# A decoder layer in one core: the quarter of the down projection with eight products goes first, and half of its tokens ahead of the other quarters

## The chip, the cores and the metric

The kernel runs on one core of one Trainium2 chip. The metric is the device time of one execution in microseconds (us), lower is better. Before the change it is 2516.35 us, the median of three runs (2516.21 to 2521.84).

The core has five engines, each with its own queue of instructions in a fixed order: PE (TensorE, matrix products; PEld in a profile is its loading of weights), DVE (VectorE), ACT (ScalarE), POOL (GpSimd) and SP (SyncE, which here issues nearly all transfers between HBM and the on-chip memory). An engine that meets an instruction whose input is not there waits, and all that stands behind it waits too.

## What is computed

A decoder layer with three sublayers, each followed by a layer norm: a retention-like self attention, a cross attention, and a gated feed-forward network. The change touches the last of these:

```python
gate = jnp.einsum('bsd,hd->bsh', x, w_gate)
up = jnp.einsum('bsd,hd->bsh', x, w_up)
gated = jax.nn.silu(gate) * up
return jnp.einsum('bsh,dh->bsd', gated, w_down)
...
x = _layernorm(x + _L0_ffn_ref(x, L0_ffn_w_gate, L0_ffn_w_up, L0_ffn_w_down), axis=-1)
```

There are 800 tokens (8 x 100), the model dimension is 1024, the hidden dimension 4096, all in fp32.

## The kernel before

**Layout.** Tokens stand along the free dimension, in two halves of N = 400. The dimension of the model is 8 blocks of 128 partitions (KT = 8), the hidden dimension 32 blocks (NHID). An fp32 product is made of three matmuls on parts: each operand is split into a high part (rounded, on ACT, line 67) and a low part (the rest, on DVE, line 68), and `mm3` (lines 85 to 88) adds high x high, high x low and low x high. Hence lines 86, 87 and 88 in every view.

**Seven products for eight.** `seven` (lines 337 to 401) multiplies a 2 x 2 block of weights with a 2 x 2 block of activations (two halves of the inner dimension, two halves of the tokens) with seven block products in place of eight, in the manner of Strassen and Winograd. It needs sums of weight blocks (DVE, lines 370 to 373) and sums of activation blocks, the tiles t1 to t4 beside b11, b21 and b22. One such unit is 7 x 4 x 3 = 84 matmuls. With `into` it adds its results into the rows y (lines 355 and 364). `proj` (lines 100 to 105) is the direct way: 8 x 3 = 24 matmuls for one block of 128 outputs and one half of the tokens, so 48 for both.

**The feed-forward part.** The up projection runs over 16 units u of two hidden blocks each: gate by `seven`, silu, up by `seven`, then the gating product (line 847) and `combine` (lines 854 to 874). `combine` stores the hidden activations to HBM, split in high and low: in the long form (t1 to t4 are computed, two kinds of splits, four stores into `hd`: 1400, 200, 400 and 800 KB), or in the short form for the direct products (one split, two stores of 800 KB into `h3d`, lines 858 to 861).

The down projection takes the hidden dimension in four quarters q of eight blocks (QT = 4 units each). Three quarters (q = 0, 1, 2) go by seven products: `down_unit(q, m)` for m = 0, 2, 4, 6, with seven chunks of 1600 KB each (lines 912 to 915), loaded from `hd`. The last quarter, q = 3, goes by the direct way, in the loop at lines 971 to 979: for each half of the tokens, for each m, 24 matmuls, an addition into y (line 976), a sum over rows (`add_up`, line 253), and then the layer norm of that half (`norm_root`, lines 275 to 287, `scaled`, lines 268 to 273). The norm of half 0 lies beside the direct products of half 1; that of half 1 is the tail of the kernel.

**What sets the order.** `in_turn` (lines 403 to 414) interleaves the steps of following units, up and down units in one list, so that the products of the next unit fill the waits of the one before. The program is then ordered by a scheduler that runs a time model of its own. Within one engine the order that results is fixed.

**Where chunks lie.** `slots` (line 903) is a ring of places: one of pool fp (tag f), z, z, four big, z. In `after_up`, behind the last up unit, pools ff (the tiles r, h, t of `combine`) and sp (temporaries) are closed, the second half of y is loaded (line 897), pool hk with two more places (tag h) is opened in the memory that became free, and these two are put at the head of the ring (lines 895 to 900). The first chunk of q = 0 is loaded into f already after unit 4 (line 891), the others when the first down unit is made (line 944), the seven of the next quarter behind unit m = 2 (lines 952 and 953). The four tiles for the direct products are taken after m = 2 of q = 2 (lines 955 to 958).

Buffers that matter: raw weights `wst` 3, split weights `w` 4, accumulator banks a 3, s 4, v 1.

Of the kernel before, what the change touches and what calls it, by code (L numbers as in the profile page):

```python
# [11 lines left out]
ALU = mybir.AluOpType  # L12
# [8 lines left out]
KT = D // P  # L21
QT = KT // 2
# [11 lines left out]
UNITS = NHID // 2  # L34
# [5 lines left out]
def decoder_layer(ctx, tc, xT, cT, w1, wo1, w2, wo2, wc, w3, wd, gw, qw, kw, trig, dec, mask, out):  # L40
    nc = tc.nc

    def sbuf(name, bufs, side=None):
        return tc.tile_pool(name=name, bufs=bufs, side=side, reuse_waits="tile")
# [8 lines left out]
    def bank(tag):  # L53
        return ps.tile([P, 512], F32, tag=tag, name=tag, bufs=banks[tag])

    def f32(ap):
        return ap.bitcast(F32)
# [4 lines left out]
    def split(dst, src):  # L62

        split2(dst[:, 0], dst[:, 1], src)

    def split2(hi, lo, src):
        nc.scalar.copy(hi, src)  # L67
        nc.vector.tensor_tensor(lo, src, f32(hi), ALU.subtract)  # L68
# [21 lines left out]
    def mmw(acc, w, k, rh, rl, start, stop):  # L90
        c = slice(k * P, (k + 1) * P)
        mm3(acc, w[:, 0, c], w[:, 1, c], rh, rl, start, stop)
# [3 lines left out]
    def acc_tag():  # L96
        turn[0] += 1
        return "as"[turn[0] % 2]

    def proj(w, z, n=N, tag="a"):  # L100
        acc = bank(tag)[:, :n]
        for k in range(KT):
            t = z[k // QT]
            mmw(acc, w, k, t[:, 0, k % QT, :n], t[:, 1, k % QT, :n], k == 0, k == KT - 1)
        return acc
# [54 lines left out]
    hd = dr.tile([QT - 1, 7, P, 2, QT, N], FR, name="hd")  # L160
    h3d = dr.tile([4, P, 2, QT, N], FR, name="h3d")
# [89 lines left out]
    def add_up(s1, y, m):  # L251
        if m > 0:
            nc.vector.tensor_tensor(s1, y[:, 0] if m == 1 else s1, y[:, m], ALU.add)
# [69 lines left out]
    def load_raw(src):  # L323
        st = wp.tile([P, KT * P], F32, tag="wst", name="wst", bufs=3)
        if isinstance(src, list):
            for i, s in enumerate(src):
                nc.sync.dma_start(out=st[:, i * H:(i + 1) * H].rearrange("p (u c) -> p u c", u=QT), in_=s)
        else:
            nc.sync.dma_start(out=st, in_=src)
        return st  # L330

    def w_split(src):
        w = wp.tile([P, 2, KT * P], FR, tag="w", name="w", bufs=4)
        split(w, src)
        return w
# [67 lines left out]
    def in_turn(units):  # L403

        at = sorted((7 * i + 2 * j, i) for i in range(len(units)) for j in range(-1, 7))
        started = {}
        for _, i in at:
            make, then = units[i]
            if i not in started:
                started[i] = make()  # L410
            try:
                next(started[i])
            except StopIteration:
                then()


    with sbuf("l1", 2) as p:
# [120 lines left out]
        def unit(h, i, then):  # L538
            c = {}
            return (lambda: seven(p, w1[h, i], w1[h, i + 1], zb, "ass", temp, c.__setitem__),  # L540
                    lambda: then(h, [(hb, c[name]) for hb, name in zip(HB, C)]))
# [76 lines left out]
    with sbuf("l2", 2) as p:  # L618
        for kv in range(NKV):
            for i0, i1 in ((0, 4), (4, 6)) if kv == 0 else ((0, 2), (2, 4), (4, 6)):  # L620
# [8 lines left out]
                for half in range(2):  # L629
                    bs = slice(half * NB, (half + 1) * NB)  # L630
                    for i in range(i0, i1):
                        acc = proj(ws[i - i0], z1[half], tag=acc_tag())
# [22 lines left out]
    with sbuf("cx", 2) as p, sbuf("c1", 1) as p1:  # L655
# [6 lines left out]
        for b in range(B):  # L662
            if b > 0:
                load_context(b)
            for kv in range(NKV):
                if early:
                    kall, row = early.pop(0)
                else:
# [7 lines left out]
                q = p.tile([P, 4, 2, T], FR, tag="q", name="q")  # L676
                nc.sync.dma_start(out=f32(q).rearrange("p h l t -> p h (l t)"),
                                  in_=f32(qd[kv, :, :, b]).rearrange("h p l t -> p h (l t)"))
# [27 lines left out]
                for j, c in enumerate(ORDER):  # L706
                    rows, n, t0 = (R6, N6, T6) if c == 6 else (P, N, 0)
# [35 lines left out]
                for j in (1, 0, 2, 3, 4, 5, 6):  # L743
                    c = ORDER[j]
                    n = N6 if c == 6 else N
# [26 lines left out]

    fp = ctx.enter_context(sbuf("fp", 1, "right"))
    z2p = ctx.enter_context(sbuf("z2", 1, "right"))
    zb = {}
# [57 lines left out]
    ORDER7 = ("b11", "b21", "b22", "t1", "t3", "t2", "t4")  # L835
# [18 lines left out]
    def combine(u, r):  # L854
        h = ff.tile([P, 7, N], FR, tag="h", name="h")
        q, j = u // QT, u % QT
        if q == QT - 1:
            split2(h[:, 0:4], r, r)
            nc.sync.dma_start(out=f32(h3d[:, :, 0, j]).rearrange("c p n -> p c n"), in_=f32(h[:, 0:4]))
            nc.sync.dma_start(out=f32(h3d[:, :, 1, j]).rearrange("c p n -> p c n"), in_=r)  # L860
            return
        t = ff.tile([P, 4, N], F32, tag="t", name="t")
        pairs = r.rearrange("p (i x) n -> p i x n", x=2)
        nc.vector.tensor_tensor(t[:, 0:2], pairs[:, :, 1], r[:, 0:2], ALU.subtract)
        nc.vector.tensor_tensor(t[:, 2], r[:, 3], t[:, 0], ALU.subtract)
        nc.vector.tensor_tensor(t[:, 3], r[:, 2], t[:, 2], ALU.subtract)
        split2(h[:, 3:7], t, t)
        split2(h[:, 1:3], r[:, 2:4], r[:, 2:4])
        split2(h[:, 0], r[:, 0], r[:, 0])
        to = lambda a, b, l: f32(hd[q, a:b, :, l, j]).rearrange("c p n -> p c n")  # L870
        nc.sync.dma_start(out=to(0, 7, 0), in_=f32(h))
        nc.sync.dma_start(out=to(0, 1, 1), in_=r[:, 0:1])
        nc.sync.dma_start(out=to(1, 3, 1), in_=r[:, 2:4])
        nc.sync.dma_start(out=to(3, 7, 1), in_=t)
# [13 lines left out]

    def after_up(u):
        if u == QT:  # L890
            load_chunk(0, down_order[:1])
        elif u == UNITS - 2:
            load_y(fp)
        elif u == UNITS - 1:
            ffpool.__exit__(None, None, None)
            sppool.__exit__(None, None, None)
            load_y(ctx.enter_context(sbuf("yy", 1)))
            pools.append(sbuf("hk", 1))
            hk = pools[0].__enter__()
            slots[0:0] = [lambda: hk.tile([P, 2, QT, N], FR, tag="h", name="h", bufs=2)] * 2  # L900
# [3 lines left out]
    down_order = ("b11", "b21", "t2", "t3", "t1", "t4", "b22")  # L904
    chunk = {}
    y2 = []

    def next_slot():
        slots.append(slots.pop(0))
        return slots[-1]()  # L910

    def load_chunk(q, names):
        for name in names:
            chunk[q, name] = next_slot()
            nc.sync.dma_start(out=f32(chunk[q, name]), in_=f32(hd[q, ORDER7.index(name)]))

    def load_y(pool):
        for _ in range(2):
            m = 2 * len(y2)
            y2.append(pool.tile([P, 2, 2 * N], F32, tag="y", name="y", bufs=2))  # L920
            for half in range(2):
                nc.sync.dma_start(out=y2[-1][:, :, half * N:(half + 1) * N], in_=zd2[half, :, m:m + 2])
# [11 lines left out]
    def down_w(q, m):  # L934


        w = wd[q * QT:(q + 1) * QT, m // QT].rearrange("u p c -> p u c")
        c = m % QT * 2 * P
        return [w[:, :, c + i * P:c + (i + 1) * P] for i in range(2)]

    def down_unit(q, m):
        def make():
            if m == 0 and q == 0:
                load_chunk(0, down_order[1:])
            z = {name: chunk[q, name] for name in ORDER7}
            into = {"c%d%d" % (i + 1, j + 1): y2[m // 2][:, i, j * N:(j + 1) * N] for i in range(2) for j in range(2)}
            return seven(fp, down_w(q, m), down_w(q, m + 1), z, "ass", into=into)

        def then():
            if m != 2:  # L950
                return
            if q < QT - 2:
                load_chunk(q + 1, down_order)
            else:
                for half in range(2):
                    z3.append([next_slot() for _ in range(2)])
                    for i in range(2):
                        nc.sync.dma_start(out=f32(z3[half][i]), in_=f32(h3d[2 * i + half]))
        return make, then

    for name in C:
        gated_block(0, name, None)
    z3 = []
    in_turn([unit(u) for u in range(1, UNITS) for unit in (gate_unit, up_unit)]
            + [down_unit(q, m) for q in range(QT - 1) for m in range(0, KT, 2)])
    pools[0].__exit__(None, None, None)


    ln_exp()
    with sbuf("ln3", 2, "right") as lnp:  # L970
        for half in range(2):
            y = rows(half)
            s1 = lnp.tile([P, N], F32, tag="s1", name="s1", bufs=2)
            for m in range(KT):
                acc = proj(w_split(load_raw(down_w(QT - 1, m))), z3[half], tag=acc_tag())
                nc.vector.tensor_tensor(y[:, m], y[:, m], acc, ALU.add)
                add_up(s1, y, m)
            r = norm_root(y, s1, lnp, idle_pe=half == 1)
            scaled(y, r, lambda m, half=half: out[:, m, half * N:(half + 1) * N])
# [71 lines left out]
```

## Time and profile before

| | us |
|---|---|
| median of the runs | 2516.35 (2516.21 to 2521.84) |
| execution that was profiled | 2522.74 |
| its span | 2521.0 |
| PE busy | 2471.7 |
| DVE busy | 1997.9 |
| ACT busy | 1352.4 |
| last down-projection matmul begins | about 2497.2 |

A line of the timeline gives start and duration in us, engine, line of the kernel, operation, output <- input, count, and in brackets the idle time before it with what ended it. A line of the waits gives engine, tile and line, what was waited for, and then total us, number and longest. In the table of windows each engine has its busy time and number of instructions in that stretch; then follow the granted clock of PE (1.00 is full), the busy share of the DMA engines and GB/s. SPq is SP's queue of transfers; the time of such a line is that of the issue, not of the transfer.

### The profile page before, as it was taken

Reading aid. Unit: us, or ns where it says so; the run is one execution under the profiler, and the core shown is the slowest. Engines: PE = TensorE matmul, PEld = TensorE weight load, DVE = VectorE, ACT = ScalarE, POOL = GpSimd, SP = SyncE. Lnnn points to the kernel's source line nnn. Section 1 sums busy time; section 2 is a strip of 40 time slices with the busy share of each in tenths; the row PEclk is TensorE's granted clock in tenths of the full one; section 3 lists DMA queues with packets and bytes.
Section 4 is the critical chain, followed back from the end, with each engine's and each line's share of the span. In section 5 each row is a group of like instructions: output and inputs, shape, how many; then the busy total and the mean of one; then the engine's idle time right before and its main releaser. Section 6 shows DMA issues by size and latency. Waiting matters only on the chain.

```text
span 2521.0 us, 37223 instructions
## 1 busy us (share of the span) xinstructions
PE 2471.7 (98%) x14042; PEld 2444.5 (97%) x14042; DVE 1997.9 (79%) x3106; ACT 1352.4 (54%) x2272; POOL 478.5 (19%) x234
## 2 busy tenths in 40 slices
PE   8999999999899999999999999999999999999997
PEld 8999999999899999999999999999999999998996
DVE  7678876568989799999999999867987777666655
ACT  6667676335767456556656556533554444432222
POOL 0111111002655344433433433100000000000000
PEclk9999999999999999999999999999999999999998
DMA  7333445774444654555555554574454444397742
GB/s 240 110 110 127 136 144 187 238 270 147 141 154 134 203 180 137 177 165 161 168 165 154 168 179 150 178 275 147 160 179 176 164 170 158 120 325 290 256 134 78
DMA packets 232898, 438.16 MB, mean 174 GB/s; under 512 B 47594, under 2 KB 176490, under 8 KB 220302
## 3 DMA queue, kind: packets, MB, share of 16 engines
q1 hardware_dynamic: 231566, 431.59, 51.0%
q0 software_dynamic: 1152, 4.19, 1.0%
q8 instruction: 110, 1.80, 0.3%
q14 instruction: 70, 0.57, 0.1%
HBM read 326.38 MB, written 109.35 MB: 173 GB/s over the span
## 4 chain that ended last, share of the span: by engine, by line
PE 89%; DVE 6%; DMA 1%; issue 1%; ACT 1%; SPq 0%; DVEq 0%; ACTq 0%
PE a L88 18%; PE a L86 18%; PE a L87 18%; PE s L88 10%; PE s L87 9%; PE s L86 9%; PE v L87 2%; PE v L88 2%; PE v L86 2%; PE s L486 1%; PE s L683 1%; DVE r L120 1%; DVE r L119 1%; PE s L148 1%; DMA tp<-in_xT 1%
## 5 line engine op out<-in xcount | busy, mean ns | idle before, releaser
L86 PE MATMUL a<-big,w 128*128 128x400 f32 (+2 forms) x1824 | 617.1, 339 | 11.2 <-ACT big L67 6.9
L87 PE MATMUL a<-big,w 128*128 128x400 f32 (+2 forms) x1824 | 616.8, 338 | 0.0
L88 PE MATMUL a<-big,w 128*128 128x400 f32 (+2 forms) x1824 | 615.4, 338 | 0.0
L67 ACT CAST w<-wst 128x1024 fp32r<-128x1024 f32 (+1 forms) x243 | 251.8, 1039 | 428.2 <-PE s L88 152.3
L68 DVE TENSOR_TENSOR w<-wst,w 128x1024 fp32r<-128x1024 f32 (+1 forms) x243 | 295.4, 1218 | 118.6 <-ACT w L67 117.3
L86 PEld LDWEIGHTS a<-big,w 128*128 128x128 f32 x1824 | 344.4, 189 | 13.1 <-ACT big L67 7.3
L87 PEld LDWEIGHTS a<-big,w 128*128 128x128 f32 x1824 | 344.9, 189 | 1.4 <-DVE big L68 0.3
L88 PEld LDWEIGHTS a<-big,w 128*128 128x128 f32 x1824 | 345.0, 189 | 0.9 <-DVE w L68 0.2
L86 PE MATMUL s<-big,w 128*128 128x400 f32 x680 | 236.0, 347 | 0.1
L87 PE MATMUL s<-big,w 128*128 128x400 f32 x680 | 234.7, 345 | 0.0
L88 PE MATMUL s<-big,w 128*128 128x400 f32 x680 | 234.6, 346 | 0.0
L125 POOL PARTITION_ALL_REDUCE ss<-sq x56 | 161.1, 2882 | 336.9 <-DMA zd<-y 167.3
L600 POOL PARTITION_ALL_REDUCE kss<-ksq x64 | 170.6, 2665 | 118.1 <-ACT ksq L599 116.4
L86 PE MATMUL a<-z,w 128*128 128x400 f32 x504 | 174.1, 345 | 8.1 <-ACT r L118 4.3
L88 PE MATMUL a<-z,w 128*128 128x400 f32 x504 | 174.9, 347 | 0.7 <-DVE w L68 0.7
L87 PE MATMUL a<-z,w 128*128 128x400 f32 x504 | 174.8, 347 | 0.0
L87 PE MATMUL s<-z,w 128*128 128x400 f32 x416 | 144.6, 348 | 2.5 <-DVE z L68 2.5
L86 PE MATMUL s<-z,w 128*128 128x400 f32 x416 | 145.3, 350 | 0.0
L88 PE MATMUL s<-z,w 128*128 128x400 f32 x416 | 144.8, 348 | 0.0
L717 ACT ACTIVATE s<-s,rk 128x400 f32<-128x400 f32 x160 | 87.7, 591 | 92.0 <-DVE sm L737 66.1
L86 PEld LDWEIGHTS s<-big,w 128*128 128x128 f32 x680 | 127.6, 188 | 1.4 <-ACT w L67 0.4
L87 PEld LDWEIGHTS s<-big,w 128*128 128x128 f32 x680 | 127.6, 188 | 1.1
(277 smaller groups left out, 5561.4 us busy)
## 6 DMA issues: line engine op xcount, KB each, us to landing
wst<-in_w SPq DMA_DIRECT2D x135, 512.0 KB
w<-wcd SPq DMA_DIRECT2D x64, 1024.0 KB
wst<-in_wo SPq DMA_DIRECT2D x64, 512.0 KB
wst<-in_wd SPq DMA_DIRECT2D x80, 256.0 KB
hd<-h SPq DMA_DIRECT2D x12, 1400.0 KB
big<-o1d SPq DMA_DIRECT2D x16, 800.0 KB
qd<-d SPq DMA_DIRECT2D x32, 400.0 KB
q<-qd SPq DMA_DIRECT2D x32, 400.0 KB
```

The costliest lines, as they stand in the source:

```text
L67: nc.scalar.copy(hi, src)
L68: nc.vector.tensor_tensor(lo, src, f32(hi), ALU.subtract)
L86: nc.tensor.matmul(acc, lh, rh, start=start, stop=False, skip_group_check=chain)
L87: nc.tensor.matmul(acc, lh, rl, start=False, stop=False, skip_group_check=chain)
L88: nc.tensor.matmul(acc, ll, rh, start=False, stop=stop, skip_group_check=chain)
L119: nc.vector.scalar_tensor_tensor(q, ss, eps, q, ALU.add, ALU.mult)
L120: nc.vector.scalar_tensor_tensor(q, q, 3.0, r, ALU.subtract, ALU.mult)
L125: nc.gpsimd.partition_all_reduce(y, x, P, op)
L148: nc.tensor.transpose(tr[0:T, b * P:(b + 1) * P], vt[:, b * T:(b + 1) * T], ident)
L486: nc.tensor.matmul(bt(o)[:, b], vv[:, b * P:(b + 1) * P], pf[:, b], start=True, stop=True)
L600: nc.gpsimd.partition_all_reduce(ss[:, at], sq[:, at], P, RED.add)
L717: nc.scalar.activation(sc, sp, AF.Copy, scale=rk[:, c:c + 1])
```

## The change

The quarter that goes by direct products becomes the first one, q = 0 (units 0 to 3), and its two halves of tokens are parted. Half 0 (`direct(0, m)` for all m) stands between the up projection and the seven-product quarters, which are now q = 1, 2, 3. Half 1 stays at the end, where the loop over halves runs its direct products with the norms. `in_turn` is called twice, once for the up units and once for the down units. The tile loaded early into f is now the first of the direct quarter; its second takes the next place of the ring, the first of hk; the seven chunks of q = 1 follow.

```diff
-        if q == QT - 1:
+        if q == 0:
             split2(h[:, 0:4], r, r)
...
-        to = lambda a, b, l: f32(hd[q, a:b, :, l, j]).rearrange("c p n -> p c n")
+        to = lambda a, b, l: f32(hd[q - 1, a:b, :, l, j]).rearrange("c p n -> p c n")
...
         if u == QT:
-            load_chunk(0, down_order[:1])
+            load_direct(0, 1)
...
+    def load_direct(half, blocks=2):
+
+        for i in range(len(z3[half]), blocks):
+            z3[half].append(next_slot())
+            nc.sync.dma_start(out=f32(z3[half][i]), in_=f32(h3d[2 * i + half]))
...
-            if m == 0 and q == 0:
-                load_chunk(0, down_order[1:])
...
         def then():
-            if m != 2:
-                return
-            if q < QT - 2:
-                load_chunk(q + 1, down_order)
-            else:
-                for half in range(2):
-                    z3.append([next_slot() for _ in range(2)])
-                    for i in range(2):
-                        nc.sync.dma_start(out=f32(z3[half][i]), in_=f32(h3d[2 * i + half]))
+            if m == 2:
+                if q < QT - 1:
+                    load_chunk(q + 1, down_order)
+                else:
+                    load_direct(1)
         return make, then
...
-    z3 = []
-    in_turn([unit(u) for u in range(1, UNITS) for unit in (gate_unit, up_unit)]
-            + [down_unit(q, m) for q in range(QT - 1) for m in range(0, KT, 2)])
+    z3 = [[], []]
+    in_turn([unit(u) for u in range(1, UNITS) for unit in (gate_unit, up_unit)])
+
+    def direct(half, m):
+        acc = proj(w_split(load_raw(down_w(0, m))), z3[half], tag=acc_tag())
+        y = rows(half)
+        nc.vector.tensor_tensor(y[:, m], y[:, m], acc, ALU.add)
+
+    load_direct(0)
+    load_chunk(1, down_order)
+    for m in range(KT):
+        direct(0, m)
+    in_turn([down_unit(q, m) for q in range(1, QT) for m in range(0, KT, 2)])
...
             for m in range(KT):
-                acc = proj(w_split(load_raw(down_w(QT - 1, m))), z3[half], tag=acc_tag())
-                nc.vector.tensor_tensor(y[:, m], y[:, m], acc, ALU.add)
+                if half == 1:
+                    direct(half, m)
                 add_up(s1, y, m)
```

More of the change, by code (lines that the diff above doesn't have):

```diff
@@ L914, in load_chunk @@
             chunk[q, name] = next_slot()
-            nc.sync.dma_start(out=f32(chunk[q, name]), in_=f32(hd[q, ORDER7.index(name)]))
+            nc.sync.dma_start(out=f32(chunk[q, name]), in_=f32(hd[q - 1, ORDER7.index(name)]))
+    def load_direct(half, blocks=2):
+        for i in range(len(z3[half]), blocks):
+            z3[half].append(next_slot())
+            nc.sync.dma_start(out=f32(z3[half][i]), in_=f32(h3d[2 * i + half]))
     def load_y(pool):
```

## The prediction

> **What bounds the kernel now.** I read the page first: how busy each engine is, and the chain that ended last.
>
> ```profile
> span 2521.0 us, 37223 instructions
> PE 2471.7 (98%) x14042; PEld 2444.5 (97%) x14042; DVE 1997.9 (79%) x3106; ACT 1352.4 (54%) x2272; POOL 478.5 (19%) x234
> PE 89%; DVE 6%; DMA 1%; issue 1%; ACT 1%; SPq 0%; DVEq 0%; ACTq 0%
> ```
>
> TensorE sets the time, and the change neither adds nor removes a matmul: the down projection keeps twelve units of seven products (84 matmuls each) and 16 direct products of 24. So only PE's idle time can move. The second view is the table of windows (first column the stretch, then its length, then busy time and count by engine, granted clock, DMA share, GB/s) over the end of the up projection and the down projection:
>
> ```profile
> core 0: us, PE busy (x) PEld busy (x) DVE busy (x) ACT busy (x) POOL busy (x), PEclk, DMA share, GB/s
> 2200.00:2250.00 50.00, 50.00 (x276) 50.00 (x275) 34.94 (x47) 18.91 (x24) 0.00 (x0) 1.00 0.79 290
> 2250.00:2300.00 50.00, 48.95 (x264) 47.29 (x262) 31.04 (x47) 10.44 (x13) 0.00 (x0) 1.00 0.96 336
> 2300.00:2350.00 50.00, 46.81 (x242) 45.95 (x241) 32.07 (x46) 10.90 (x13) 0.00 (x0) 0.93 0.62 215
> 2350.00:2400.00 50.00, 50.00 (x276) 50.00 (x275) 34.55 (x50) 12.98 (x14) 0.00 (x0) 1.00 0.77 277
> ```
>
> A full stretch of 50 us holds 276 matmuls, 0.181 us each. Between 2250 and 2350 there are 506 instead of 552: 46 x 0.181 = 8.3 us lost, with DMA at its limit just before. The timeline of PE shows the largest piece, the third bracket being the idle time before the matmul:
>
> ```profile
> 2320.25 0.70 PE L86 MATMUL s<-f,w 128*128 128x400 f32 x1 [3.19 <-ACT w L67]
> 2320.74 0.54 PE L87 MATMUL s<-f,w 128*128 128x400 f32 x1
> ```
>
> That is all there is to win here. What can be lost is in the third view, the timeline of SP's queue at the change from up to down (start, duration of the issue, line, transfer), with the vector engine's last gating product of the up projection and the one wait of that queue that matters:
>
> ```profile
> 2240.46 0.57 DVE L847 TENSOR_TENSOR r<-a,s 128x400 f32<-128x400 f32 x1 [1.49 <-PE a L88]
> ...
> 2236.98 3.40 SPq L915 DMA_DIRECT2D big<-hd  x2
> 2240.47 0.38 SPq L915 DMA_DIRECT2D z<-hd  x1
> 2242.62 0.37 SPq L859 DMA_DIRECT2D h3d<-h  x1
> 2244.98 0.37 SPq L860 DMA_DIRECT2D h3d<-r  x1
> 2249.60 9.56 SPq L327 DMA_DIRECT2D wst<-in_wd  x4
> 2260.88 2.64 SPq L922 DMA_DIRECT2D y<-zd  x4
> 2263.56 0.94 SPq L915 DMA_DIRECT2D h<-hd  x2
> ```
>
> ```profile
> SPq L922 <- DMA h3d<-r: 1.7, 1, 1.7
> ```
>
> The last product of the up projection ends at 2240.4. The tiles of pool hk take the memory of pools ff and sp, so the first load into them waits for the last store out of ff. That store is issued at 2244.98 and lands only at 2260.9, because the seven chunk loads stand before it; the hk loads go out at 2263.56, 23.1 us after the last up product. Before the change nobody needs them: they belong to the second quarter, and PE first reads an h tile at 2286.5.
>
> **The Trainium skill.** "DMA: Bandwidth & Descriptors", section "Queues, rings and completion order", says that SP owns one row of rings, that each DMA engine consumes it in ring order, and that completion is nevertheless not strictly in order. The trace agrees with the first part: 15.9 us for 0.8 MB behind loads. "TensorE: Matmul & The Clock Gate", section "What's actually happening", says that about 3.4 us of idleness halve the clock and about as much work restores it. The trace agrees: after 3.19 us idle some 16 matmuls came 0.333 us apart.
>
> **The change, part by part.** I use the instruction order of the changed kernel as built, priced with rows of this trace. Up to the first chunk load (2214.21, when the last up unit has used b11) PE's order has the same number of instructions, so the times before it are kept.
>
> (1) Combine. Units 0 to 3 now take the short form (two splits, two stores), units 12 to 15 the long one. After the last up product the long form costs DVE, from the rows by form: 0.57 gate, 0.98, 0.57 and 0.57 for t, 0.57, 0.99 and 1.82 for the low parts, together 6.1 us; then its four stores, 2.87 MB (1400 + 800 + 400 + 200 KB) in place of 1.64. Units 0 to 3 get as much back, where PE is full: nothing.
>
> (2) When the last up product ends. Before, 36 matmuls of the first down unit stand ahead of it, after, only 11 of the first direct product: 25 x 0.181 = 4.5 us earlier, about 2235.8.
>
> (3) The direct half. Each of its eight products needs z3[0] in two tiles. The first lies in f since unit 4. The second is the first new slot, a tile of hk. PE's order behind the last up product is 37 matmuls on f (the rest of m = 0 and the first halves of m = 1 to 3), then m = 0 on the hk tile. Nothing else can be put before it: the four w buffers hold m = 0 to 3, and m = 4's weights need m = 0's buffer. So PE stops at 2235.8 + 37 x 0.181 = 2242.5 unless the hk tile is there.
>
> (4) When it is there. SP's order is: chunk loads of z, z, four of big, z (also one of the next quarter), with weights for m = 2 to 5 and the stores of units 14 and 15 between, then the weights of m = 6, four y loads (which wait for the r and h stores), the hk load (which waits for the t store). Bytes from the first chunk load to the t store: 7 x 1.64 = 11.5, 4 x 0.52 = 2.1, 2 x 2.87 = 5.7, together 19.3 MB. Before, the same stretch was 7 x 1.64 chunks, seven weight halves of 0.26, four stores of 0.82, together 16.6 MB from 2212.65 to 2260.9: 0.344 MB per us. So the t store lands at about 2213 + 19.3 / 0.344 = 2269. It cannot be issued before the DVE end of 2242. Behind it 1.64 MB of hk and what is left of y (1.64) and weights (0.52): 4.4 us (hk alone) to 10.1 us (all 3.8 MB) at 0.375 MB per us, the mean of 2214 to 2268; I take 8, since part of y can go while the t store is under way. The tile is there at 2277: PE idles 34.5 us. The bounds: 6 us if nothing stands before them (t store at 2242, 0.82 / 0.375 = 2.2 for it and 4.4 for the load: 2248.6), 42 if the load behind it, 1.64 MB, shares with it and SP issues late.
>
> (5) The clock after it: 16 x (0.333 - 0.181) = 2.4 us.
>
> (6) Recovery. In the idle time the remaining chunk loads drain, and the order of the later quarters is regular again, without the runs of two matmuls that the old order had around 2250 to 2350. I take all of the 8.3 us as gained (bounds 0 and 8.3). Between quarters an old tile comes free every 4.4 us and is 1.64 MB: 0.37 MB per us, at the limit but not over it, as from 2350 to 2380 before, without loss.
>
> (7) The end. The first half's sums of rows now wait only for the last down unit; on PE a matmul with the mean waits for it, some 1.4 us idle, against 1.3 now ("PE s L278" waiting for DVE). In DVE's order two additions instead of one stand after the last product: +0.6 us on the 23.6 us of the tail. The other DMAs (z3 for the end: two loads instead of four) are hidden by the last down units.
>
> The sum: +34.5 + 2.4 - 8.3 + 0.6 = +29.2 us, on this execution 2521.0 + 29.2 = 2550.2. The execution with profile took 2522.74 us in all and stands 6.4 above the median of the runs, 2516.35; the same difference on the median gives 2545.5. About 0.3% (7.5 us) is what a measurement of this kernel can tell from no change.
>
> **Rivals.** (A) As above, with 25 to 42 us of idle time: 2536 to 2553. For it: the 15.9 us of a small store and the 23.1 us to the hk load are measured in the same place with less in the queue.
>
> (B) The queue is shallower than its bytes: the stores pass the loads (the page on DMA leaves completion out of order open), and the hk tile is there 6 to 24 us after PE stops. Sum at 16: +16 + 2.4 - 8.3 + 0.6 = +11, 2527; at 6, +1, 2517. Against it: the store of 2244.98 did not pass.
>
> (C) The other side, faster: the hk tile does not hang on the last unit's stores, because its place was free before. Then the direct half is 35 us of work (192 x 0.181) with two tiles only, in which the first seven-product quarter loads unseen, and the 8.3 us are won: 2516.35 - 8.3 + 0.6 = 2508.6. It decides where the hk load goes out before about 2237. Against it: the 1.7 us in which the load ahead of it waits for the store.
>
> (D) Longer: SP's issue itself is pushed back (four weight halves took 9.56 us), so y, hk and the weights of m = 7 come one after another, and a second wait of some 10 us follows: 2560.
>
> (E) The order is not what is said (no direct half ahead): it is in the built order, so I give it nothing.
>
> **Numbers.** A 0.73, B 0.13, C 0.05, D 0.09. The time is A's, 2545.5. The range 2522 to 2560 holds A, more than half of B and half of D. Faster: C with little else, 0.06. Within 0.3%: the low end of B, 0.06. Slower: 0.88.
>
> **What would show it.** Right: one idle stretch of PE of over 20 us near 2243, ended by a DMA into h, DMA at its limit through it; the y loads at about 2262 to 2270 in SP's queue; granted clock down in the window after; full windows of 276 from there to the end, and the tail about 24 us. Wrong: the hk load issued before 2250; PE idle in several small pieces or between quarters; or losses of 8 us still found in the later quarters.

## The result, and the profile after

| | before | after |
|---|---|---|
| median of four runs, us | 2518.69 (2516.21 to 2521.84) | 2554.86 (2552.38 to 2559.32) |
| execution that was profiled, us | 2522.74 | 2554.74 |
| its span, us | 2521.0 | 2553.0 |

The ratio is 1.0142, with a 95% interval of 1.0129 to 1.0154: the change costs 36.2 us by the medians and 32.0 us between the two profiled executions.

The page of the changed kernel, first lines and chain that ended last:

```profile
span 2553.0 us, 37231 instructions
PE 2471.0 (97%) x14042; PEld 2444.4 (96%) x14042; DVE 2000.1 (78%) x3106; ACT 1353.8 (53%) x2272; POOL 480.4 (19%) x234
PE 84%; DVE 8%; DMA 3%; ACT 2%; issue 2%; SPq 1%; POOL 0%; DVEq 0%; ACTq 0%
```

PE does the same 14042 instructions in the same busy time; its share of the chain that ended last falls from 89% to 84%, while DMA and DVE gain two points each and the others at most one. Where that is, the table of windows says (columns as before: stretch, length, PE, PEld, DVE, ACT, POOL with counts, granted clock, DMA share, GB/s):

```profile
2200.00:2250.00 50.00, 44.67 (x236) 43.44 (x234) 31.34 (x40) 18.60 (x23) 0.00 (x0) 0.97 0.78 277
2250.00:2300.00 50.00, 20.74 (x100) 20.69 (x101) 11.95 (x15) 6.24 (x7) 0.00 (x0) 0.66 0.79 286
2300.00:2350.00 50.00, 50.00 (x276) 50.00 (x275) 33.04 (x48) 12.04 (x13) 0.00 (x0) 1.00 0.40 131
2350.00:2400.00 50.00, 50.00 (x277) 50.00 (x276) 32.60 (x47) 11.34 (x12) 0.00 (x0) 1.00 0.84 303
2400.00:2450.00 50.00, 50.00 (x276) 50.00 (x275) 34.49 (x49) 13.46 (x14) 0.00 (x0) 1.00 0.77 271
2450.00:2500.00 50.00, 49.95 (x275) 49.62 (x274) 32.24 (x47) 13.06 (x13) 0.00 (x0) 1.00 0.30 85
```

From 2200 to 2300 us there are 336 matmuls where 552 fit. At 0.1813 us each (331 in 60 full us), the 216 that are missing are 39.2 us lost in one place. From 2300 to 2500 us all stretches are full; of the 8.3 us that the kernel before loses between 2250 and 2350, the 34 matmuls missing after 2300 (6.2 us) are not lost here. Over 2200 to 2350 us as a whole the loss is 39.2 us for 8.3. The timeline of PE (the bracket is the idle time and what ended it) has three gaps in it:

```profile
2243.66 0.51 PE L86 MATMUL a<-f,w 128*128 128x400 f32 x1 [3.00 <-ACT w L67]
2244.92 0.70 PE L88 MATMUL a<-f,w 128*128 128x400 f32 x1 [0.41 <-DVE w L68]
2279.26 0.70 PE L86 MATMUL s<-h,w 128*128 128x400 f32 x1 [31.17 <-DMA h<-h3d]
```

The third is the half's second operand tile. What it waited for is read from the chain of waits before that matmul (start, us, what):

```profile
2231.91 14.50 DMA big<-hd
2246.48 8.58 SPq L873
2255.15 0.96 SPq L874
2256.21 1.04 SPq L872
2257.34 11.95 DMA hd<-t
2269.30 9.91 DMA h<-h3d
```

and from the timeline of SP's queue around it:

```profile
2238.44 5.25 SPq L916 DMA_DIRECT2D big<-hd  x2
2243.78 0.38 SPq L916 DMA_DIRECT2D z<-hd  x1
2244.26 1.85 SPq L327 DMA_DIRECT2D wst<-in_wd  x2
2246.48 8.58 SPq L873 DMA_DIRECT2D hd<-r  x1
...
2257.34 2.95 SPq L875 DMA_DIRECT2D hd<-t  x1
2260.39 3.13 SPq L327 DMA_DIRECT2D wst<-in_wd  x2
2263.62 4.61 SPq L929 DMA_DIRECT2D y<-zd  x4
2269.30 0.33 SPq L922 DMA_DIRECT2D h<-h3d  x1
```

(In the program's names `big`, `z` and `h` <- `hd` are block loads of a seven-product quarter, called chunks in the description above; `hd` <- `r`, `h`, `t` are the stores of a unit, `wst` <- `in_wd` are weights, and `h` <- `h3d` is the tile.) The lines show the order of the queue: block loads of the next quarter, then the last unit's four stores, then y, then the one tile that TensorE needs next, with weights between them. The stores' data were all ready when DVE ended at 2242.9, but the first of them is issued at 2246.5 and the last at 2257.3. The tile's load goes out in the moment in which the last store lands.

### The profile page after: what moved, and what is told of

It is laid out like the page before. It is cut to its first block, busy times and chain, and to the rows that moved or that the text cites. A ratio compares the mean times of both kernels' runs of the same rounds, so it can differ in the third digit from the quotient of the medians.

```text
span 2553.0 us, 37231 instructions
## 1 busy us (share of the span) xinstructions
PE 2471.0 (97%) x14042; PEld 2444.4 (96%) x14042; DVE 2000.1 (78%) x3106; ACT 1353.8 (53%) x2272; POOL 480.4 (19%) x234
## 4 chain that ended last, share of the span: by engine, by line
PE 84%; DVE 8%; DMA 3%; ACT 2%; issue 2%; SPq 1%; POOL 0%; DVEq 0%; ACTq 0%
PE a L88 17%; PE a L86 17%; PE a L87 17%; PE s L88 9%; PE s L87 9%; PE s L86 9%; PE v L88 1%; PE v L86 1%; PE v L87 1%; PE s L486 1%; DVE r L120 1%; PE s L683 1%; DMA cs<-in_cT 1%; DMA rr<-row 1%; DVE w L68 1%
## 5 line engine op out<-in xcount | busy, mean ns | idle before, releaser
L86 PE MATMUL a<-big,w 128*128 128x400 f32 (+2 forms) x1792 | 605.9, 339 | 9.2 <-ACT big L67 6.5
L87 PE MATMUL a<-big,w 128*128 128x400 f32 (+2 forms) x1792 | 605.9, 338 | 0.2 <-DVE big L68 0.2
L88 PE MATMUL a<-big,w 128*128 128x400 f32 (+2 forms) x1792 | 604.5, 338 | 0.0
L86 PEld LDWEIGHTS a<-big,w 128*128 128x128 f32 x1792 | 338.3, 189 | 10.5 <-ACT big L67 6.8
L87 PEld LDWEIGHTS a<-big,w 128*128 128x128 f32 x1792 | 339.1, 189 | 1.7 <-DVE big L68 0.8
L88 PEld LDWEIGHTS a<-big,w 128*128 128x128 f32 x1792 | 339.2, 190 | 0.9 <-DVE w L68 0.3
L86 PE MATMUL s<-big,w 128*128 128x400 f32 x648 | 224.7, 347 | 0.0
L87 PE MATMUL s<-big,w 128*128 128x400 f32 x648 | 223.7, 345 | 0.0
L88 PE MATMUL s<-big,w 128*128 128x400 f32 x648 | 223.7, 346 | 0.0
L86 PE MATMUL a<-z,w 128*128 128x400 f32 x520 | 180.0, 346 | 10.5 <-ACT r L118 5.6
L88 PE MATMUL a<-z,w 128*128 128x400 f32 x520 | 180.8, 348 | 0.7 <-DVE w L68 0.7
L87 PE MATMUL a<-z,w 128*128 128x400 f32 x520 | 180.4, 347 | 0.0
L87 PEld LDWEIGHTS s<-big,w 128*128 128x128 f32 x648 | 121.7, 188 | 1.0
L86 PEld LDWEIGHTS s<-big,w 128*128 128x128 f32 x648 | 121.6, 188 | 0.9
```

What stands on the lines that cost most here:

```text
L86: nc.tensor.matmul(acc, lh, rh, start=start, stop=False, skip_group_check=chain)
L87: nc.tensor.matmul(acc, lh, rl, start=False, stop=False, skip_group_check=chain)
L88: nc.tensor.matmul(acc, ll, rh, start=False, stop=stop, skip_group_check=chain)
```

## The experiments

Each run is compared with runs of the kernel before on the same chip (medians 2517.06 us for e3, e5, e6 and e7, 2517.05 for e11, e13 and e14, 2517.77 for e15, e16 and e17, 2519.08 for e20). All edits are against the changed kernel unless another base is named. The last column counts the matmuls of one profiled execution between 2200 and 2350 us; each that is missing against the kernel before is 0.1813 us. It helps because the executions differ ahead of 2200 us by up to 27 matmuls (4.9 us), a lead or lag that is there before the stretch begins.

| run | median, us | ratio to before, 95% interval | us above before | matmuls, 2200 to 2350 us |
|---|---|---|---|---|
| before | | | | 778 |
| the change | 2554.86 | 1.0142 [1.0129, 1.0154] | 36.2 | 610 |
| e7_no_last_store | 2550.84 | 1.0134 [1.0117, 1.0151] | 33.8 | 611 |
| e16_last_store_early | 2545.13 | 1.0108 [1.0093, 1.0123] | 27.4 | 665 |
| e5_operand_first | 2541.98 | 1.0099 [1.0084, 1.0114] | 24.9 | 667 |
| e11_weights_ahead | 2534.38 | 1.0063 [1.0047, 1.0079] | 17.3 | 704 |
| e13_weights_spread | 2532.07 | 1.0055 [1.0037, 1.0072] | 15.0 | 694 |
| e14_blocks_last | 2531.79 | 1.0055 [1.0038, 1.0071] | 14.7 | 708 |
| e6_other_place | 2529.81 | 1.0050 [1.0035, 1.0065] | 12.8 | 702 |
| e3_both_at_end | 2525.59 | 1.0033 [1.0020, 1.0046] | 8.5 | 738 |
| e15_blocks_last_store_early | 2522.94 | 1.0020 [1.0009, 1.0030] | 5.2 | 754 |
| e17_at_end_store_early | 2521.44 | 1.0015 [1.0006, 1.0024] | 3.7 | 767 |
| e20_before_blocks_later | 2519.45 | 1.0005 [0.9997, 1.0013] | 0.4 | 777 |

### Both halves at the end again

```diff
-        if u == QT:
-            load_direct(0, 1)
+        if u == 2 * QT:
+            load_chunk(1, down_order[:1])
...
-    in_turn([unit(u) for u in range(1, UNITS) for unit in (gate_unit, up_unit)])
+    in_turn([unit(u) for u in range(1, UNITS) for unit in (gate_unit, up_unit)]
+            + [down_unit(q, m) for q in range(1, QT) for m in range(0, KT, 2)])
...
-                if half == 1:
-                    direct(half, m)
+                direct(half, m)
```

> The first quarter is still the one by eight products, with its operand stored in the short form, and the last unit before the down projection still has the long combine and the 2.87 MB of hd stores; but both halves of the eight products stand at the end again and the three quarters by seven follow the up products in one list. My theory (the cost is that the half ahead hangs on one operand tile whose place is freed only by the last unit's stores, so TensorE stops for 31 us): the 31 us wait is gone, and the time is that of the kernel before within its noise, 2515 to 2524 us. Rival 1 (the longer combine and the larger stores at the end of the up products cost by themselves): 2528 us or more, with TensorE waiting at the start of the down projection. Rival 2 (the quarter's place among the stores and loads matters, not where its halves stand): as slow as the changed kernel, 2550 us or more.

Measured: 2525.59 us, 8.5 above before. The 31 us wait is gone, but the time lies between what the theory and rival 1 gave. TensorE's waits in it:

```profile
PE s L86 <- ACT w L67: 8.1, 3, 3.2
```

Three waits for split weights, where the kernel before has one of 3.2 us (and one of 0.3). So the exchange of the quarters alone, without the half ahead, has a price. What goes with it is the longer combine and 2.87 MB of stores in place of 1.64 for each of the last units; a later run without the last unit's stores looks at the second. Rival 2 falls. The other 28 us come with the half ahead.

### The tile's load ahead of the blocks

The block loads of q = 1 and the last weights of the half were pinned behind the tile in SP's order; three blocks come before the weights of m = 7, four after.

```diff
...
     load_direct(0)
-    load_chunk(1, down_order)
+    load_chunk(1, down_order[:3])
     for m in range(KT):
         direct(0, m)
+    load_chunk(1, down_order[3:])
```

> The changed kernel with the order of SyncE's issues pinned after the last unit's stores: the four y loads, the half's second operand tile, then three blocks of the next quarter, the weights of the half's last row block, then the other four blocks. In the changed kernel six block loads of 1.64 MB stand ahead of those stores in the queue. My theory (of the 31 us the larger part is backlog: block loads in front of the stores that free the place, 8.6 us of issue standing still and a store that takes 12 us to land): the wait for the tile falls to 8 to 16 us, and the time to 2530 to 2542 us; part may come back as waits for the blocks of the next quarter at 2275 to 2290 us, since they start later. Rival (the chain from the last up product through combine, store, place and load is long in itself, whatever is in the queue): the wait stays at 25 to 33 us and the time at 2548 us or more.

Measured: 2541.98 us, 24.9 above before where the change has 36.2. TensorE's waits and SP's queue in this run:

```profile
PE s L86 <- DMA h<-h3d: 17.1, 1, 17.1
PE a L86 <- ACT w L67: 8.2, 2, 7.0
```

```profile
2242.01 0.36 SPq L877 DMA_DIRECT2D hd<-t  x1
2243.21 5.14 SPq L935 DMA_DIRECT2D y<-zd  x4
2249.30 0.33 SPq L926 DMA_DIRECT2D h<-h3d  x1
2249.68 0.45 SPq L918 DMA_DIRECT2D h<-hd  x1
2250.17 1.40 SPq L918 DMA_DIRECT2D z<-hd  x3
```

With no block load before them the last store is issued 15.3 us earlier (2242.0 for 2257.3), and the tile is there 21.1 us earlier (2258.2 for 2279.3). This execution is some 1.8 us ahead already at 2200 us (10 matmuls more), so 13.5 and 19.3 us are the better numbers. Backlog was 14 of the 31 us of the wait; 17 remain for combine, store, y loads and the load itself, just above the range expected, while the time is at its upper end. The rival, a wait of 25 us or more whatever is in the queue, falls. The blocks started late, and TensorE waited 7.0 us until 2294 for weights that stand behind them; the expectation had looked for a wait on the blocks themselves, earlier.

### The wait on the stores taken away

```diff
-        nc.sync.dma_start(out=to(0, 7, 0), in_=f32(h))
...
+        if u == UNITS - 1:
+            return
+        for j in ([j, j + 1] if u == UNITS - 2 else [j]):
+            ...
+            nc.sync.dma_start(out=to(0, 7, 0), in_=f32(h))
```

> The changed kernel, but the last unit's results are not stored; instead the unit before it stores its own results twice, into its own place and into the last unit's (so a sixteenth of the product over the hidden rows takes the wrong values; the bytes and the number of transfers are the same). The tile's place is then free once the last combine is done (about 2243 us), and no store is behind the block loads. My theory (dependency and backlog both): the wait falls by the time from the stores' issue to their landing less what the block loads in front still hold up the tile's load itself: 12 to 20 us remain, 2534 to 2543 us. Rival 1 (bandwidth alone: the same bytes must move before the tile is there): the wait stays at 27 to 33 us and the time at 2550 us or more. Rival 2 (the stores alone are the wait, the queue is no matter): 8 us or less remain, 2530 us or less.

Measured: 2550.84 us, 33.8 above before, against 36.2 for the change; the two ratios' intervals overlap, so no difference is established, and in the stretch the two profiles have 611 and 610 matmuls. The tile's place no longer hangs on any store of the last unit, and still:

```profile
PE s L86 <- DMA h<-h3d: 22.5, 1, 22.5
PE a L86 <- ACT w L67: 11.9, 2, 10.8
```

```profile
2236.25 13.80 DMA big<-hd
2250.12 9.63 SPq L932
...
2263.10 11.64 DMA h<-h3d
```

The tile came at 2274.8 us for 2279.3, but this execution is 4.0 us ahead already at 2200 us (22 matmuls more): measured by the work done, the tile came about as late as before. The wait for it is shorter because weights for the fourth row block, now behind the doubled stores, came later and held TensorE for 10.8 us: 33.3 us for the two waits, where the change has 34.2 (31.2 + 3.0). (The other 1.1 us of the second line lie near the end of the kernel.) The chain no longer holds a store; a block load and the y loads stand in its stead. My theory, in which about half of the wait was the stores, falls here, and rival 1 (the bytes that must go first) takes its place. Of its two numbers the time holds; the tile's own wait is below its range of 27 to 33 us, and with the wait for weights just above it.

### Another place for the tile

```diff
-            slots[0:0] = [lambda: hk.tile([P, 2, QT, N], FR, tag="h", name="h", bufs=2)] * 2
+            slots[7:7] = [lambda: hk.tile([P, 2, QT, N], FR, tag="h", name="h", bufs=2)] * 2
```

The second tile then goes to a z place, and its load is issued at 2212.4 us. The places that come free last go to the blocks needed last.

> The changed kernel with one number of the list of places changed: the half's second operand tile goes into a place that an operand of the last up product leaves (a z place) and the places that wait for the last unit's stores go to the last block of the next quarter and to the quarter after it. My theory: no wait for the tile any more; TensorE runs on into the eight products. The weights of the last row blocks and the y loads still stand behind block loads and stores in SyncE's queue, so I expect waits of 8 to 25 us in sum on weights or on the last block at 2250 to 2300 us, and 2522 to 2540 us. Rival 1 (the parting of the list, with its drain and refill, costs the 30 us, whichever tile is waited for): 2548 us or more, the idle time only changes its name. Rival 2 (the two other costs in the changed kernel, cold clock and the tail, are larger than I took them): a time above before by more than TensorE's idle time shows.

Measured: 2529.81 us, within the range expected. No wait for an operand tile is left; the waits are for weights:

```profile
PE a L86 <- ACT w L67: 7.3, 1, 7.3
PE s L86 <- ACT w L67: 6.5, 2, 4.2
```

14.6 us with the two small ones on DVE (0.6 and 0.2). Rival 1 falls: parting the list is not what costs 30 us. Rival 2 is not seen in the time, 12.8 us above before, less than the waits. From 2200 to 2300 us 122 matmuls are missing, 22.1 us, more than the waits, since half clock follows them; but as in the change nothing is lost from 2300 to 2350 us.

### Three orders of the queue on that kernel

As in the last run, and five of the block loads pinned behind other rows' weights:

```diff
...
-    load_chunk(1, down_order)
+    load_chunk(1, down_order[:2])
     for m in range(KT):
         direct(0, m)
+        for i in {5: (2, 3, 4, 5, 6)}.get(m, ()):
+            load_chunk(1, down_order[i:i + 1], True)
```

For the second order the table is `{5: (2, 3), 6: (4,), 7: (5, 6)}`, for the third `{7: (2, 3, 4, 5, 6)}`.

> The run with the other place, and on top of it the order of SyncE's issues changed: five of the seven block loads of the next quarter are pinned behind the weights of the half's sixth row block, so the weights of row blocks 4 and 5 go ahead of four block loads (6.6 MB) instead of behind them; the last unit's stores and the weights of row blocks 6 and 7 stay behind those loads. Theory (what was left of the loss in the run with the other place, 14.6 us of waits for weights and the half clock after them, is weights that lie behind block loads in the same queue): the waits on weights fall to 0 to 6 us, and the time from 2530 to 2510 to 2522 us. Rival 1 (the transfers are at their rate: whatever goes first, the same bytes are missing later): the wait only moves, to the blocks of the next quarter or to the weights of rows 6 and 7, and the time stays at 2526 to 2534 us. Rival 2: the weights can't go earlier, since their staging tiles are not free: as rival 1 in time, with SyncE waiting on VectorE ahead of those loads.

> As the run with the weights ahead, but the block loads are spread: two behind the weights of row block 5, then the last unit's stores, then one block load behind the weights of row block 6 and one behind those of row block 7. Theory (order in the queue): no wait on weights over 2 us, all cover of 35 us kept, 2508 to 2518 us, below the kernel before. Rival (the transfers' rate): waits on the blocks of the next quarter at 2270 to 2290 us instead, of 8 to 16 us, and 2524 to 2532 us.

> As the run with the weights ahead, but five block loads (8.2 MB) stand behind all weights of the half, so they start at about 2245 us and the transfers are idle for some us before that. Theory (order in the queue; 8.2 MB at 0.34 MB/us are there at about 2270 to 2278 us, and TensorE comes to them at about 2272): no wait on weights, a wait of 0 to 8 us on the blocks, 2510 to 2522 us. Rival (the transfers' rate): the idle time of the transfers is lost, so this is the slowest of the three orders, 2530 us or more.

Measured: 2534.38, 2532.07 and 2531.79 us, none below the 2529.81 of the run they start from. The theory that these orders of the queue would win what was left falls three times. TensorE's waits for weights are 17.9, 17.9 and 16.7 us; they are moved, not removed. The rivals (the rate of the transfers) come nearer, with the first two times at most 0.4 us above their ranges, but not in all they said: TensorE waits for no block in any of the three, and the third order is not the slowest. In the third order TensorE runs without a gap up to 2266 us, and then waits 7.4 and 9.3 us. The chain of that run shows why:

```profile
2243.34 9.08 DMA wst<-in_wd
2252.46 19.90 DMA wst<-in_wd
2272.38 13.91 DMA wst<-in_wd
```

Three weight transfers of 0.26 MB, each from its issue to its landing, are all the chain from 2243 to 2286 us. The first was issued behind the last unit's stores, the second behind four block loads, the third behind the y loads and two blocks. And over the whole stretch the transfers are busy throughout in all of these kernels but the change, from the windows 2215 to 2300 us:

| | DMA share | GB/s | matmul instructions |
|---|---|---|---|
| before | 0.99 | 356 | 456 |
| the change | 0.90 | 321 | 253 |
| e3_both_at_end | 1.02 | 360 | 415 |
| e6_other_place | 1.03 | 366 | 346 |
| e11_weights_ahead | 1.03 | 364 | 347 |
| e13_weights_spread | 1.03 | 362 | 338 |
| e14_blocks_last | 1.02 | 365 | 352 |

The Trainium skill, "DMA: Bandwidth & Descriptors", section "Where 436 GB/s comes from", gives about 358 GB/s as the bound of transfers between HBM and the on-chip memory for one core. The 356 to 366 GB/s of the kernels that are busy throughout lie near it, but it is no ceiling here: the change moves 380 GB/s from 2215 to 2280 us, and e5_operand_first 405 from 2250 to 2300. So "full" is read from the busy share, about 1, and the rate that goes with it varies. With the half ahead, in a free place, the 31 MB that go through (85 us x 0.365 MB/us) go with 104 to 118 matmuls fewer than the 30 MB of before. The change is full as well until its tile has landed; from 2280 to 2290 us its share is 0.29, since by then the queue is drained and TensorE has fallen behind.

### Fewer bytes in the full stretch

If bytes are the bound, taking some out must help, whatever waits for what. The stores of the last unit were dropped again, but the copies that fill its place are written at the fourth unit from the end, where the transfers are half idle:

```diff
+        if u == UNITS - 1:
+            return
+        for j in ([j, j + 3] if u == UNITS - 4 else [j]):
```

The same edit was put on three kernels: the change, the third order above, and the kernel with both halves at the end.

> As the run without the last unit's stores, but the copies that fill the last unit's place are written three units before it, where the transfers are half idle, not one unit before it: so 2.87 MB less go through the full stretch from 2215 us on (again a sixteenth of the product over the hidden rows takes the wrong values). Theory (the stretch is bound by the bytes that must go through it, about 0.37 MB/us as the runs so far show): 7.8 us less idle time than in that run, 2541 to 2546 us against its 2550.8. Rival 1 (the tile's wait is the chain from the combine over its place and the y loads, and bytes are no matter): no change, 2548 to 2553 us. Rival 2 (with nothing behind them the stores' place in the queue was the whole wait): 2530 us or less.

> The run with the other place and the block loads last, with the same move of 2.87 MB of stores out of the full stretch (a sixteenth of the product over the hidden rows takes the wrong values). The three orders of that kernel gave 2532 to 2534 us whichever went first. Theory (bytes): 7.8 us less, 2521 to 2527 us. Rival (waits and issue order, not bytes): no change, 2529 to 2534 us.

> The run with both halves at the end (2525.6 us, 8.5 above before), with the same move of 2.87 MB of stores out of the full stretch (a sixteenth of the product over the hidden rows takes the wrong values). Theory (its 8.5 us over before are the 1.23 MB more that its last units store, and the rest of before's own loss is bytes as well): 2516 to 2520 us, at or just below before. Rival (the longer combine, on VectorE and ScalarE, is what costs there): 2523 to 2527 us.

Measured, as us above before: 27.4, against 33.8 with the copies late; 5.2, against 14.7; 3.7, against 8.5. So 2.87 MB less go with a gain of 6.4, 9.5 and 4.8 us. At 0.365 MB/us they are 7.9 us. The first two lie in the ranges expected; the third, 2521.44, lies above its range of 2516 to 2520, and below the rival's 2523 to 2527, so about half of what was to be explained there goes with the stores, and the rest is open (weights still stand behind block loads in it, and the transfers are at 122 GB/s between 2270 and 2280 while TensorE waits).

The pair e16 and e7 is the clearest: the same matmuls in the same order through the stretch, and the last unit's stores left out of both; only when the copies are written differs. The waits of e16, to be set against those of e7 above:

```profile
PE s L86 <- DMA h<-h3d: 21.1, 1, 21.1
PE a L86 <- ACT w L67: 4.5, 2, 3.4
```

In the stretch that is 24.5 us for 33.3, and 54 matmuls more. In the other two pairs TensorE's order differs too, and with the last unit's stores left out nothing waits for them any more, so there the gain is not bytes alone. In all three the bytes left the stretch together with their issues on SP; these two were not told apart.

### A version below both

The kernel before loses 8.3 us between 2250 and 2350 us. The block loads of its second quarter were put behind one more unit's weights (base: the kernel before):

```diff
...
+            if q == 1 and name in down_order[:2]:
+                tc.keep_in_program_order(put)
...
-            if m != 2:
+            if m != (4 if q == 0 else 2):
```

> The kernel before (the quarter by eight products last), with the first block loads of its second quarter issued one unit of two row blocks later, two of them pinned behind the weights of that unit, so that 0.52 MB more of weights go ahead of 3.3 MB of blocks in the full stretch. The kernel before loses 8.3 us of matmul time between 2250 and 2350 us, with a 3.2 us wait for weights among it. Theory (in the full stretch it is bytes and their order that stop TensorE): the wait for weights goes, 2510 to 2515 us, a version below both kernels. Rival 1 (the bytes are the limit, the order moves the wait only, as in the three orders tried on the changed kernel): 2515 to 2519 us. Rival 2 (the blocks now come late for the second quarter): 2522 us or more.

Measured: 2519.45 against 2519.08 us, ratio 1.0005 [0.9997, 1.0013], no change. Rival 1 holds (its range ended at 2519, and the kernel before itself is at 2519.08 on this chip): the wait for weights is now

```profile
PE s L86 <- ACT w L67: 5.5, 1, 5.5
```

Between 2250 and 2300 us 11 matmuls are won, between 2300 and 2350 us 12 are lost: the loss has moved. No version below the kernel before was found.

## Why the prediction was right, step by step

The forecast was 2545.5 us in a range of 2522 to 2560; measured 2554.86.

- **(1) and (2).** The last gating product begins at 2236.19 and the long combine ends at 2242.94: 6.75 us for 6.1; the difference is 0.7 us in which DVE waits between its steps. The last up product ends about 2236.1, for 2235.8.
- **(3) The cover.** TensorE did stop on the tile after the work on f. What the step left out is the 3.00 + 0.41 us before the fourth row block: its weights lie behind a block load and land only at 2242.5, so the last 12 matmuls on f ran late and most of them at half clock, and the stop came at 2248.1 for 2242.5.
- **(4) The tile.** The last store was to land at 2269 and did at 2269.3; the y loads at 2262 to 2270, they went out at 2263.6; the tile at 2277, it was there at 2279.3. Idle time 34.5 us, measured 31.2 + 3.4 = 34.6. The sum of bytes over the rate was the right working, but the numbers are closer than their parts. To the landing of the last store the traces moved 17.6 MB before and 20.5 MB after, at 0.366 and 0.365 MB/us; the step has 16.6 and 19.3 MB and 0.344. Some weights are missing on both sides, so the error cancels (and the 0.375 for 2214 to 2268 us is 0.370). The tile's own load took 10.0 us for 8, while a block load issued 0.4 us behind it shared the transfers: 4.1 MB moved in that time. That the idle time fits to 0.1 is luck: the tile was 2.3 us late, and half clock delayed the stop by 2.2. The reason that the step names beside the sum, that the load waits for the last store out of ff, is in the chain but isn't the price: with no store of the last unit to wait for, e7 shows no established difference. The tile waits for the bytes ahead of it, and the stores are one part of them.
- **(5) Clock.** The 216 matmuls lost are 39.2 us; less the 34.6 of waits this leaves 4.6 for half clock, for 2.4: two stretches of it, not one. The prediction's remark that its trace agrees with 3.4 us in both directions is too kind: the idle time there was 3.19 us, and half clock lasted 5.8 us (2320.25 to 2326.03).
- **(6) Recovery.** No matmul is missing from 2300 to 2450 us, so the 8.3 us can be set against the 39.2, as taken.
- **(7) The end.** Wrong in sign: from the last matmul of the down projection to the end of the span it is 23.35 us (2529.65 to 2553.0), 0.6 less than before (2497.05 to 2521.0), though the mean waits 1.8 us now for 1.3.

Together 39.2 - 8.3 - 0.6 = 30.3 of the 32.0 us between the spans. Of the other 1.7, a wait of 1.14 us for weights at 2501, among the direct products of half 1, is new, and 0.4 us lie ahead of 2200 (two matmuls fewer by then). The sum of the steps, 29.2, was 2.8 short. The larger miss is the step from the profiled execution to the median: 6.4 us were taken off, since the profiled one stood that far above the median of three. With a fourth run that median rose by 2.3, and the profiled execution of the changed kernel stands 0.1 below its median. Without that step the text's own sum gives 2522.7 + 29.2 = 2551.9 (2550.2 as a span).

**Of the rivals**, B (stores that pass the loads) is not seen: the last store took 12.0 us to land, and the tile came 31.2 us after the stop, not 6 to 24. D had the issue that is pushed back (8.58 us for one store), but no second wait behind it came. C's premise, a tile whose place was free before, was tried as e6_other_place: 12.8 us above before where C gave 8 below. Its error is in "the first seven-product quarter loads unseen": with the transfers full (share 1.03 in e6), TensorE waited 14.6 us there.

**What the 36 us are.** About 8.5 is the exchange of the quarters with its larger stores (e3). With the half ahead and the tile in a place that was free, in any order tried, it is 13 to 17; so the half ahead costs 4 to 9 more. By their sizes its loads are 5.8 MB in the full stretch (a tile of 1.64 and eight weights of 0.52), in place of the weights of the seven-product units that stood there; that this is the price was not tested by itself. The rest, 19 to 23 us, is that the change put the one tile that everything hangs on at the end of the queue. That the floor of 13 to 17 is mostly the load on the transfers is supported by the three orders that came out alike and by the stores moved out, which took 9.5 of 14.7 us away; it is not shown that no other order would do better, and which bytes would have to go to reach the kernel before was not tried further.

## What to carry to other kernels

Before moving work into a gap, add up the bytes that this work needs by then, and set them against the transfer rate in that stretch: independent work covers a load only if the bytes ahead of it can move in the meantime. With the transfers full here, giving the first needed tile the last place in the queue cost 19 to 23 us; better orders won that back and no more, and beyond that only fewer bytes in the stretch helped. A dependency that ends a wait last in the chain is not yet its price: take it away and see whether the next thing in the same queue ends it as late.

## What the runs showed of the hardware

The issue of a transfer on SP took much longer in the full stretch than elsewhere. All issues of one kind of store in the changed kernel (duration in ns: shortest, median, longest; the 200 KB store of the r tile):

```profile
L873 SPq DMA_DIRECT2D hd<-r x12: 326/327/8580, 1909.4 to 2246.5; - x12
```

It took 0.33 us as a rule and 8.58 for the last unit's store in the full stretch, and what stands behind it in the queue was issued only when it had ended (2255.15 us).

An idle time of 3.00 us was enough for half clock: of the 12 matmuls after it, those without a wait of their own before them came 0.29 to 0.34 us apart (one 0.50) until 3.7 us after the first, then 0.18. In e3_both_at_end even 2.46 us were enough (the wait that ends at 2250.53 us; the matmuls ahead of it came 0.18 us apart, those after it 0.33).

Half clock lasted 3.4 us after this wait, 5.5 us after the 31.17 us of the change, and 5.8 us after the 3.19 us of the kernel before. The Trainium skill, "TensorE: Matmul & The Clock Gate", section "What's actually happening", says that at least one idle window of about 3.4 us goes ahead of the half clock and about as much busy time ends it; the waits here were shorter and some stretches of half clock longer, and the measured values are the ones to plan with.
